# A second stage buffer, freer row buffers and a new static order in a graph-attention and slice-attention kernel

## The chip, the cores and the metric

The kernel runs on one core of a Trainium2 chip. The metric is the device time of one execution in microseconds (us). The core has five engines that matter here: TensorE (PE in the profile, with its weight loads as PEld), VectorE (DVE), ScalarE (ACT), GpSimd (POOL) and the queue of SyncE (SP), from which nearly all DMA transfers are issued.

## The reference, cut to what matters

x has 32 batches of 512 nodes with 256 features, all float32. Each batch is independent of the others; `adj` is shared. One layer is two residual blocks:

```python
def _gat(inp, adj_mask, W, a):
    h = inp @ W
    f1 = h @ a[:F_, 0];  f2 = h @ a[F_:, 0]
    e = leaky_relu(f1[:, :, None] + f2[:, None, :], 0.2)
    if adj_mask is not None:
        e = where(adj_mask > 0, e, NEG_INF)
    att = softmax(e, axis=2)
    return elu(einsum('bij,bjf->bif', att, h))

def gnn(x, ...):                                  # 256 -> 512 -> 256 features
    out = relu(x @ mlp1_w + mlp1_b);  residual = out
    out = elu(_gat(relu(out), None, W_fc, a_fc)) + residual
    out = relu(out @ mlp2_w + mlp2_b); residual = out
    return relu(elu(_gat(relu(out), adj, W_hand, a_hand)) + residual)

def ffn(x, ...):                                  # 8 heads, 64 slices of 64 features
    slice_weights = softmax((x_mid @ W_slice + b_slice) / temp)
    slice_token = einsum(fx_mid, slice_weights) / (sum(slice_weights) + 1e-5)
    # ... attention among the 64 slices of each head: q, k, v, softmax
    out_x = einsum(out_slice, slice_weights)
    return out_x @ W_out + b_out

x = x + gnn(layernorm(x), adj, ...)
x = x + ffn(layernorm(x), ...)
```

## The kernel before

The kernel does not run its instructions in the order in which they are written. `Recorder` first notes every operation of all 32 batches. It then gives each operation a key (the batch times a period, plus the turn of its step, plus corrections for the first three and the last three batches), and lays all operations out in one static order for each engine, with a list scheduler that starts, on each engine, the ready operation with the smallest key. Work of two to four batches is interleaved in this way. The chip then follows that fixed order, each engine by itself, and waits on semaphores where data or a buffer is not there yet.

A tile is given a buffer of its tag. The scheduler hands the buffers of a tag out in a fixed sequence of tiles: one sequence over all batches, or, for PSUM tiles and tags that begin with "stage", one sequence inside each batch, with the batches free against each other:

```python
class _Log:
    def __init__(self, ap, age):
        tensor = ap.tensor
        self.name, self.tag, self.bufs = tensor.name, tensor.tag, tensor.tag_meta.bufs
        self.psum = ap.space == bass.MemoryType.PSUM
        self.queue = self.tag, age if self.psum or self.tag.startswith("stage") else 0
```

`age` is the batch. The tiles `u` and `m` are rows of 512 elements with two buffers each; they serve in the first attention (pv) and in the second one (pv2). A tag carries the name of its pool after the tile's own, so the tags of these rows begin with "u_" and "m_".

A matrix is transposed either on TensorE, into PSUM, or in three parts: VectorE transposes 32x32 blocks into a stage tile (`flip`), four DMA transfers write the stage to DRAM, and one reads it back in the final order:

```python
EDGES = (0, B - 1)
Q = 32
def flip(src, dst):
    nc.vector.transpose(dst, src.rearrange("p (c i) -> p c i", i=Q))
def by_dma(what, b):
    return what in FLIPPED and b not in EDGES    # FLIPPED = xn, u, e, o2, w, xn2, s1
def gather(what, stage, dst):
    blocks, width = stage.shape[1:]
    scr = dram.tile([blocks, Q, P // Q, width], F32, name="scr", tag=f"scr_{what}", bufs=2)
    for a in range(P // Q):
        nc.sync.dma_start(scr[:, :, a, :].rearrange("c r j -> r c j"), stage[ts(a, Q), :, :])
    nc.sync.dma_start(dst, scr.rearrange("(k c) r a j -> (c r) k (a j)", c=P // Q))
```

The first and the last batch (`EDGES`) take TensorE's way instead, for all but o2. One batch goes through these steps (loops over tiles cut to one line, the TensorE branches for the edges cut):

```python
# load, norm1: xt from DRAM; layernorm on VectorE, with its power on GpSimd; xn flipped, gathered as xnT
# mlp1: 8 matmuls of 512 columns -> o0T (relu on ScalarE)
# h: 32 matmuls of 257 columns, weights wfc -> h (copies on ScalarE)
# factors, p: 5 transposes; two exponentials and four row products -> pT
nc.step = "pv"                               # first attention, 32 matmuls
o1T = new("o1T", [P, KH, N])
if by_dma("u", b):
    stage = new("u_stage", [P, HID // Q, P], tag="stage")
for i in range(NT):
    # ... pms: two PSUM tiles, pT x h
    u, m = row("u"), row("m")
    elu_elu([...], m, u)                     # VectorE and ScalarE in turn, 6 operations
    if by_dma("u", b):
        flip(u, stage[:, :, ts(i, Q)]); continue
nc.step = "o1"
gather("u", stage, o1T)
for m in range(KH):                          # + o0T, on VectorE
    nc.vector.tensor_tensor(o1, o1, swapped(o0T[:, m, :]), op=OP.add)

nc.step = "mlp2"                             # 8 matmuls of 512 columns
o2T = new("o2T", [P, KD, N])
# ... nc.scalar.activation(o2T[:, m, :], pm, AF.Relu, bias=...)
nc.step = "h2"                               # 8 matmuls of 258 columns, 4 transposes (f2b)
nc.step = "e"
if by_dma("e", b):
    stage = new("e_stage", [P, N // Q, P], tag="stage")
for i in range(NT):                          # 3 VectorE operations, exp on ScalarE, then:
    flip(e, stage[:, :, ts(i, Q)])
nc.step = "p2"
gather("e", stage, pT)                       # pT is p2T here
# ... o2T flipped and gathered as r2; x loaded again as x1
nc.step = "pv2"                              # second attention, 16 matmuls in two halves
u, m = row("u2", (P, 2, D), "u"), row("m2", (P, 2, D), "m")
# ... elu_elu, + r2, + x1

nc.step = "norm2"
layernorm(x1, xn, "ln2")                     # xn is xn2 here
raw = new("xn2_raw", [P, KD, N], tag="raw4")
transpose_features("xn2", b, xn, raw, True)  # 4 flips, gather; then ScalarE copies raw into xn2T
nc.step = "w"                                # 8 matmuls of 512 columns (weff, xn2T), softmax over 64
stage_w = new("w_stage", [P, INNER // Q, P], tag="stage")
# ... 4 flips; later gathered as w_raw and copied into wT
nc.step = "sums"                             # 16 matmuls of 257 columns (xn2, w) -> s1, flipped, gathered as s1T
nc.step = "tokens"                           # small matmuls: s1T x wfx, nrow x bfx, tok x wqk, scores (tok, qbd)
nc.step = "att"; "vo"; "gg"                  # softmax over 64 slices, transposes, attT x tokbd, 4 matmuls gg
attT = new("attT", [P, NP, G])
nc.step = "out"                              # 16 matmuls gg x wT, added to x1, written out
```

A DMA that is issued from the SP queue and has a wait stands in that queue until the wait is over; those behind it stand too.

Of the kernel before, what the change touches and what calls it, by code (L numbers as in the profile page):

```python
# [13 lines left out]
ENGINES = ("tensor", "vector", "scalar", "gpsimd", "sync")  # L14

TURNS = {
    "load": -145.1, "norm1": -102.2, "mlp1": 176.5, "h": 203.5, "factors": 206.6, "p": 209.3,
    "pv": 219.9, "o1": 240.0, "mlp2": 243.4, "h2": 273.9, "e": 274.6, "p2": 274.6,
    "pv2": 305.6, "norm2": 314.1, "w": 376.2, "sums": 378.3, "s1T": 396.3, "tokens": 446.2,
    "att": 472.7, "vo": 472.7, "gg": 472.7, "out": 483.8,  # L20
}
PERIOD, SPARE = 92.2, 0.00

HEAD = (
    (-8, -8, 49, -10, -8, 25, 0, -39, -4, 6, -2, -2, -40, -2, -2, -2, -2, -2, 3, -8, 1, -20),
    (8, 2, 25, 1, 1, 0, 8, 8, 1, 1, -7, 0, 2, 2, 2, 2, 2, 2, 2, -5, 9, 2),
    (0, -1, -1, 0, 0, -22, 0, 12, 0, 1, 0, 0, 0, 0, 0, 0, 11, 0, 0, 0, -3, 0),
)
TAIL = (
    (0, 0, 53, 0, 0, 0, 0, 4, 0, 0, -6, 2, 0, 0, 0, 0, 2, 0, 3, 3, -5, 4),  # L30
    (0, 0, 17, 1, -2, -27, 0, -2, -4, -38, 0, 23, 1, -6, -2, 9, 2, 6, -2, -2, -2, -2),
    (-85, 1, 1, 1, 1, 16, 20, 22, 19, 19, 19, 7, 14, -7, 9, 9, -7, 0, -7, 0, -16, -30),
)


# [2 lines left out]
FLIPPED = ("xn", "u", "e", "o2", "w", "xn2", "s1")  # L38

P = 128  # L40
# [235 lines left out]
# [5 lines that stand above are left out]
        self.name, self.tag, self.bufs = tensor.name, tensor.tag, tensor.tag_meta.bufs  # L281
        self.psum = ap.space == bass.MemoryType.PSUM

        self.queue = self.tag, age if self.psum or self.tag.startswith("stage") else 0
        self.entries = []


# [22 lines left out]
def adj_ffn_kernel(  # L310
# [26 lines left out]
    B, N, D = x.shape  # L337
    HID = mlp1_w.shape[1]
    HH = HID // 2
    NT = N // P  # L340
    KD = D // P
    KH = HID // P
    HEADS = temperature.shape[1]
    G = W_slice.shape[1]
    C = W_slice.shape[0]
    INNER = HEADS * C
    NP = INNER // P
# [11 lines left out]
    def new(name, shape, bufs=1, tag=None, dtype=F32):  # L359
        return sbuf.tile(list(shape), dtype, name=name, tag=tag or name, bufs=bufs)  # L360

    def mm_tile(shape):
        return psum.tile(shape, F32, tag="mm", name="mm", bufs=5)
# [4 lines left out]
    def sm_tile(shape):  # L368
        return tr_tile(shape)

    EDGES = (0, B - 1)
    Q = 32

    def flip(src, dst):
# [2 lines left out]

    def by_dma(what, b):

        return what in FLIPPED and b not in EDGES  # L380

    def gather(what, stage, dst):

# [32 lines left out]
    def load_x(b):  # L416
# [14 lines left out]
        out=ident, in_=ident, compare_op=OP.not_equal, fill=1.0, base=0,  # L431
# [160 lines left out]
    for p in range(NP):  # L592
        pv = mm_tile([P, D])
# [49 lines left out]
    def front(b):  # L643
# [5 lines left out]
        xn = new("xn", [P, NT, D])  # L649
# [15 lines left out]
        h = new("h", [P, NT, 2, HH + 1])  # L665
# [49 lines left out]
        nc.step = "pv"  # L715
        o1T = new("o1T", [P, KH, N])
        if by_dma("u", b):
            stage = new("u_stage", [P, HID // Q, P], tag="stage")
        for i in range(NT):
            pms = [mm_tile([P, HH + 1]), mm_tile([P, HH])]  # L720
            for s, pm in enumerate(pms):
# [7 lines left out]
            u, m = row("u"), row("m")  # L729
# [13 lines left out]
        if by_dma("u", b):  # L743
            gather("u", stage, o1T)
            for m in range(KH):
                o1 = o1T[:, m, :].rearrange("p (t a i) -> p t a i", t=NT, i=Q)
# [3 lines left out]
    def middle(b, o1T):  # L750

        nc.step = "mlp2"
        o2T = new("o2T", [P, KD, N])
        for m in range(KD):
            pm = mm_tile([P, N])
            for k in range(KH):
                nc.tensor.matmul(
                    pm.rearrange("p (a t i) -> p a t i", t=NT, i=Q), w2[:, k, ts(m)],
                    swapped(o1T[:, k, :]), start=(k == 0), stop=(k == KH - 1),
                )  # L760
            nc.scalar.activation(o2T[:, m, :], pm, AF.Relu, bias=b2[:, m : m + 1])
        nc.step = "h2"
        h = new("h2", [P, NT, D + 2])
        for t in range(NT):
            pm = mm_tile([P, D + 2])
            for k in range(KD):
                nc.tensor.matmul(
                    pm, o2T[:, k, ts(t)], wh[:, k, :], start=(k == 0), stop=(k == KD - 1)
                )
            nc.scalar.copy(h[:, t, :], pm)  # L770
        f2b = tr_tile([P, N])
        for j in range(NT):
            nc.tensor.transpose(f2b[:, ts(j)], h[:, j, D + 1 : D + 2].to_broadcast([P, P]), ident)
        if not by_dma("e", b):
            pt, f2b = f2b, new("f2b", [P, N], tag="acb")
            nc.scalar.copy(f2b, pt)
        nc.step = "e"
        pT = new("p2T", [P, NT, N])
        if by_dma("e", b):
            stage = new("e_stage", [P, N // Q, P], tag="stage")  # L780
        nmax = small("nmax", [P, NT])
        for i in range(NT):
            e = new("e", [P, N], bufs=2)
            nc.vector.scalar_tensor_tensor(
                e, f2b, h[:, i, D : D + 1], mbias[:, i, :], op0=OP.add, op1=OP.add
            )
            nc.vector.scalar_tensor_tensor(e, e, ALPHA, e, op0=OP.mult, op1=OP.max)
            nc.vector.tensor_reduce(
                nmax[:, i : i + 1], e, axis=AX.X, op=OP.max, negate=True
            )  # L790
            nc.scalar.activation(e, e, AF.Exp, bias=nmax[:, i : i + 1])
            if by_dma("e", b):
                flip(e, stage[:, :, ts(i, Q)])
                continue
            pt = tr_tile([P, NT, P])
            for j in range(NT):
                nc.tensor.transpose(pt[:, j, :], e[:, ts(j)], ident)
            nc.scalar.copy(
                pT.rearrange("p j (t a i) -> p j t a i", t=NT, i=Q)[:, :, :, i, :],
                pt.rearrange("p j (t i) -> p j t i", i=Q),  # L800
            )
        nc.step = "p2"
        if by_dma("e", b):
            gather("e", stage, pT)

        nc.vector.memset(h[:, :, D], 1.0)

        r2 = new("r2", [P, NT, D])
        stage = new("o2_stage", [P, N // Q, KD * Q], tag="stage4")
        for k in range(KD):  # L810
            nc.vector.transpose(
                stage[:, :, ts(k, Q)].rearrange("p (t a) i -> p t a i", t=NT),
                swapped(o2T[:, k, :]),
            )
        gather("o2", stage, r2)

        x1 = new("x1", [P, NT, D], bufs=2)
        nc.sync.dma_start(x1, x[b].rearrange("(p t) d -> p t d", p=P))
        nc.step = "pv2"
        for i2 in range(NT // 2):  # L820
            parts = []
            for s in range(2):
                i = 2 * i2 + s
                pm = mm_tile([P, D + 1])
                for j in range(NT):
                    nc.tensor.matmul(
                        pm, pT[:, j, ts(i)], h[:, j, : D + 1], start=(j == 0), stop=(j == NT - 1)
                    )
                rd = small("rd2", [P, 1])
                nc.vector.reciprocal(rd, pm[:, D : D + 1])  # L830
                parts.append((pm[:, :D], rd, s))
            u, m = row("u2", (P, 2, D), "u"), row("m2", (P, 2, D), "m")
            elu_elu(parts, m, u)
            for s in range(2):
                u3 = u[:, s, :].rearrange("p (k a i) -> p k a i", k=KD, i=Q)
                r3 = r2[:, 2 * i2 + s, :].rearrange("p (a k i) -> p k a i", k=KD, i=Q)
                nc.vector.tensor_tensor(u3, u3, r3, op=OP.add)
            nc.vector.scalar_tensor_tensor(
                x1[:, ts(i2, 2), :], u, 0.0, x1[:, ts(i2, 2), :], op0=OP.max, op1=OP.add
            )  # L840
        return x1

    def back(b, x1):

        nc.step = "norm2"
        xn = new("xn2", [P, NT, D + 1])
# [1 line left out]
        layernorm(x1, xn, "ln2")  # L848
        xnT = new("xn2T", [P, KD, N])
        if by_dma("xn2", b):  # L850
            raw = new("xn2_raw", [P, KD, N], tag="raw4")
            transpose_features("xn2", b, xn, raw, True)
            for k in range(KD):
                nc.scalar.copy(
                    xnT[:, k, :].rearrange("p (t a i) -> p t a i", t=NT, i=Q), swapped(raw[:, k, :])
                )
        else:
            transpose_features("xn2", b, xn, xnT, False)

        nc.step = "w"  # L860
        w = new("w", [P, NT, INNER])
        wT = new("wT", [P, NP, N])
        if by_dma("w", b):
            stage_w = new("w_stage", [P, INNER // Q, P], tag="stage")
        for t in range(NT):
            pm = mm_tile([P, INNER])
            for k in range(KD):
# [28 lines left out]
        s1 = new("s1", [P, NP, D + 1])  # L896
        if by_dma("s1", b):
            stage = new("s1_stage", [P, D // Q, P], tag="stage4")
# [20 lines left out]
        if by_dma("w", b):  # L919
            raw = new("w_raw", [P, NP, N], tag="w")  # L920
# [6 lines left out]
        s1T = med("s1T", (P, KD, INNER))  # L927
# [74 lines left out]
        pt = tr_tile([P, NP, G])  # L1002
        for q in range(NP // 2):
            nc.tensor.transpose(pt[:, ts(q, 2), :], sc[:, ts(q, 2), :], ident)
        attT = new("attT", [P, NP, G])
        nc.scalar.copy(attT, pt)
        pa = mm_tile([P, NP, G])
        halves(pa, tokbd, attT)
# [2 lines left out]
        gg = med("gg")  # L1011
        for p2 in range(NP // 2):
            pg = mm_tile([P, 2, D])
            for s in range(2):
                p = 2 * p2 + s
# [87 lines left out]
```

## Time and profile before

| | |
|---|---|
| time, median of 3 runs | 2681.41 us (2673.46 to 2681.55) |
| span of the profiled execution | 2673.3 us |
| DVE busy | 2081.2 us, 78% |
| ACT busy | 1093.4 us, 41% |
| DMA moved | 375.40 MB, mean 140 GB/s |
| TensorE busy in the first 84 us, in a middle stretch of 84 us, in the last 84 us | 68.8, 82.3 (918 to 1002 us), 68.6 us |

A line of the timeline has the start, the length, the engine, the source line (here always that of the recorder), the operation, the tile written and the tiles read, the shape, and how many such instructions follow each other. In square brackets stands the idle time of the engine just before, and what ended it. "SPq" is the queue of SyncE; its lines are issues of transfers, not the transfers. A float32 matmul as written in the kernel is two records in the trace, a transpose on TensorE is one. The profile leaves out some digits of tile names: `o_stage` is o2_stage, `xn_stage` stands for the stages of xn and of xn2, `xn_raw` is xn2_raw, `h` can be h or h2. `w_raw` is the gathered w before ScalarE copies it into wT; `mm` and `tr` are PSUM tiles. So `mm<-wfc,o0T` is the step h, `mm<-xnT,w` mlp1, `mm<-h,pT` pv, `mm<-o1T,w` mlp2, `mm<-wh,o2T` h2, `mm<-s1T,wfx` and `mm<-nrow,bfx` tokens, `mm<-tok,wqk` the step after them.

### The profile page before, as it was taken

To read this page: it belongs to the slowest core of one execution; us is meant where nothing else is said; L and a number is where in the kernel's file an instruction comes from. 1 tells how busy PE (TensorE), PEld (TensorE's weight loads), DVE (VectorE), ACT (ScalarE), POOL (GpSimd) and SP (SyncE) were. 2 spreads that over 40 slices of the span, in tenths; PEclk is the share of its full clock that TensorE was granted. 3 is DMA by queue.
4 is the path that set the end of the run, shared out by engine and by line. 5 is a ranking of instruction groups with operands and counts; after the bars stand their busy time and mean duration, and the time that the engine had idled before them with its cause. 6 is when DMAs were issued, how large, how long until landed. Compare 5 with 4: busy or idle time off the path is not lost.

```text
span 2673.3 us, 35248 instructions
## 1 busy us (share of the span) xinstructions
PE 2608.7 (98%) x12477; PEld 1929.1 (72%) x12477; DVE 2081.2 (78%) x5161; ACT 1093.4 (41%) x2009; POOL 111.8 (4%) x171
## 2 busy tenths in 40 slices
PE   7999999999999999999999999999999999999997
PEld 5776667777777777777777777776777767777775
DVE  6577778877778877779877788777788777888785
ACT  3443344433444433444434444334444334444341
POOL 1000000000000000000000000000000000000000
PEclk9999999999999999999999999999999999999998
DMA  5125455554455454556554555544564545554440
GB/s 162 52 67 148 122 156 166 152 156 132 137 166 166 137 161 116 147 168 165 148 141 128 157 166 148 154 127 139 168 172 134 154 122 150 166 158 142 127 119 23
DMA packets 465657, 375.40 MB, mean 140 GB/s; under 512 B 86597, under 2 KB 382665, under 8 KB 465481
## 3 DMA queue, kind: packets, MB, share of 16 engines
q1 hardware_dynamic: 463896, 372.10, 49.6%
q8 instruction: 99, 1.62, 0.2%
q10 hardware_dynamic: 1584, 1.05, 0.1%
q14 instruction: 78, 0.63, 0.1%
HBM read 197.96 MB, written 175.11 MB: 140 GB/s over the span
## 4 chain that ended last, share of the span: by engine, by line
PE 45%; DVE 29%; DMA 16%; issue 3%; SPq 3%; POOL 2%; ACT 1%; DVEq 0%; ACTq 0%
PE mm L273 43%; DMA xt<-in_x_dram 5%; DVE u L273 4%; DVE e L273 3%; DMA o1T<-scr 3%; DMA scr<-e_stage 3%; SPq L273 3%; PE tr L273 2%; DVE w L273 2%; POOL ln_rstd L273 2%; DVE e_stage L273 2%; DVE w_stage L273 2%; DMA scr<-u_stage 2%; DVE m L273 1%; DVE u_stage L273 1%
## 5 line engine op out<-in xcount | busy, mean ns | idle before, releaser
L273 PE MATMUL mm<-wfc,o0T 128*128 128x257 f32 x2048 | 479.3, 381 | 0.0
L273 PE MATMUL mm<-h,pT 128*128 128x257 f32 (+1 forms) x2048 | 468.1, 380 | 4.2 <-DVE pT L273 4.2
L273 PEld LDWEIGHTS mm<-wfc,o0T 128*128 128x128 f32 x2048 | 381.9, 189 | 82.2 <-issue 24.8
L273 PEld LDWEIGHTS mm<-h,pT 128*128 128x128 f32 x2048 | 385.2, 190 | 64.3 <-DVE pT L273 6.7
L273 ACT COPY h<-mm 128x257 f32<-128x257 f32 (+1 forms) x384 | 142.9, 372 | 302.2 <-PE mm L273 295.8
L273 PE MATMUL mm<-xn,w 128*128 128x257 f32 x1024 | 255.1, 383 | 4.0 <-ACT w L273 3.3
L273 PE MATMUL mm<-xnT,w 128*128 128x512 f32 x512 | 240.4, 600 | 10.8 <-DMA xnT<-scr 7.3
L273 PE MATMUL mm<-gg,wT 128*128 128x256 f32 x1024 | 245.3, 379 | 0.0
L273 PE MATMUL mm<-h,p2T 128*128 128x257 f32 x1024 | 244.9, 380 | 0.3 <-ACT o0T L273 0.3
L273 PE MATMUL mm<-o1T,w 128*128 128x512 f32 x512 | 227.4, 596 | 13.4 <-DVE o1T L273 10.8
L273 PE MATMUL mm<-weff,xn2T 128*128 128x512 f32 x512 | 231.7, 595 | 0.0
L273 PEld LDWEIGHTS mm<-h,p2T 128*128 128x128 f32 x1024 | 191.4, 190 | 31.3 <-ACT o0T L273 0.7
L273 PEld LDWEIGHTS mm<-xn,w 128*128 128x128 f32 x1024 | 187.8, 191 | 35.0 <-issue 8.9
L273 PEld LDWEIGHTS mm<-gg,wT 128*128 128x128 f32 x1024 | 191.7, 190 | 28.6 <-issue 1.0
L273 PEld LDWEIGHTS mm<-o1T,w 128*128 128x128 f32 x512 | 94.8, 190 | 131.0 <-issue 94.5
L273 DVE STREAM_TRANSPOSE o_stage<-o2T 128x512 f32<-128x512 f32 x64 | 45.5, 710 | 163.6 <-ACT o2T L273 163.6
L273 ACT ACTIVATE e<-e,nmax 128x512 f32<-128x512 f32 x128 | 92.4, 722 | 186.0 <-DVE nmax L273 184.5
L273 DVE SCALAR_TENSOR_TENSOR e<-tr,h,mbias 128x512 f32<-128x512 f32 x120 | 86.6, 742 | 99.3 <-PE tr L273 99.3
L273 ACT ACTIVATE m<-m 128x512 f32<-128x512 f32 x192 | 120.9, 630 | 102.4 <-DVE m L273 102.1
L273 PEld LDWEIGHTS mm<-weff,xn2T 128*128 128x128 f32 x512 | 93.0, 191 | 92.3 <-issue 90.5
L273 PEld LDWEIGHTS mm<-xnT,w 128*128 128x128 f32 x512 | 92.2, 191 | 93.1 <-issue 72.7
L273 ACT ACTIVATE w<-w 128x512 f32<-128x512 f32 x128 | 80.7, 631 | 177.2 <-DVE w L273 177.0
(151 smaller groups left out, 3798.9 us busy)
## 6 DMA issues: line engine op xcount, KB each, us to landing
scr<-xn_stage SPq DMA_DIRECT2D x240, 128.0 KB, 2.5
scr<-u_stage SPq DMA_DIRECT2D x120, 256.0 KB, 4.1
o1T<-scr SPq DMA_DIRECT2D x30, 1024.0 KB, 6.0
scr<-e_stage SPq DMA_DIRECT2D x120, 256.0 KB, 3.8
p2T<-scr SPq DMA_DIRECT2D x30, 1024.0 KB, 5.5
scr<-w_stage SPq DMA_DIRECT2D x120, 256.0 KB, 4.6
w_raw<-scr SPq DMA_DIRECT2D x30, 1024.0 KB, 7.3
x<-in_x_dram SPq DMA_DIRECT2D x32, 512.0 KB, 5.7
```

The costliest lines, as they stand in the source:

```text
L273: getattr(getattr(self.nc, op.engine), op.method)(*op.args, **op.kwargs)
```

## The change

It gives the three stage tiles of pv, e and w, which shared one buffer, two; lets the rows u and m of different batches be handed out independently of each other; and sends the first batch's w, xn2 and s1 through DRAM instead of through TensorE. To make room in SBUF, xn2_raw moves into the buffer of o2T, and attT into that of sc2. The turns of the steps and the corrections for the first and last three batches are set anew, so that the static order differs on each engine. The purpose is an order with fewer ties between batches.

```diff
 TURNS = {
-    "load": -145.1, "norm1": -102.2, "mlp1": 176.5, "h": 203.5, "factors": 206.6, "p": 209.3,
-    "pv": 219.9, "o1": 240.0, "mlp2": 243.4, "h2": 273.9, "e": 274.6, "p2": 274.6,
-    "pv2": 305.6, "norm2": 314.1, "w": 376.2, "sums": 378.3, "s1T": 396.3, "tokens": 446.2,
-    "att": 472.7, "vo": 472.7, "gg": 472.7, "out": 483.8,
+    "load": -122.2, "norm1": 78.3, "mlp1": 267.5, "h": 296.1, "factors": 313.0, "p": 323.7,
+    "pv": 324.8, "o1": 324.8, "mlp2": 340.5, "h2": 360.8, "e": 385.5, "p2": 385.7,
+    "pv2": 430.7, "norm2": 437.4, "w": 494.8, "sums": 496.8, "s1T": 507.4, "tokens": 549.1,
+    "att": 558.0, "vo": 558.2, "gg": 560.3, "out": 593.0,
 }
-PERIOD, SPARE = 92.2, 0.00
+PERIOD, SPARE = 91.1, 0.01
 # HEAD and TAIL: corrections of the keys of each step in the first and the last three batches,
 # 3 x 22 numbers each; before -85 to 53, after -478 to 149 (cut)
@@ class _Log
-        self.queue = self.tag, age if self.psum or self.tag.startswith("stage") else 0
+        self.queue = self.tag, age if self.psum or self.tag.startswith(("stage", "u_", "m_")) else 0
@@
-    EDGES = (0, B - 1)
+    EDGES = {0: ("xn", "u", "e"), B - 1: ("xn", "u", "e", "w", "xn2", "s1")}
@@ by_dma
-        return what in FLIPPED and b not in EDGES
+        return what in FLIPPED and what not in EDGES.get(b, ())
@@ pv
-            stage = new("u_stage", [P, HID // Q, P], tag="stage")
+            stage = new("u_stage", [P, HID // Q, P], bufs=2, tag="stage")
@@ e
-            stage = new("e_stage", [P, N // Q, P], tag="stage")
+            stage = new("e_stage", [P, N // Q, P], bufs=2, tag="stage")
@@ norm2
-            raw = new("xn2_raw", [P, KD, N], tag="raw4")
+            raw = new("xn2_raw", [P, KD, N], tag="o2T")
@@ w
-            stage_w = new("w_stage", [P, INNER // Q, P], tag="stage")
+            stage_w = new("w_stage", [P, INNER // Q, P], bufs=2, tag="stage")
@@ vo
-        attT = new("attT", [P, NP, G])
+        attT = new("attT", [P, NP, G], tag="sc2")
```

## The prediction

> **What bounds the kernel now.** I read the page's first two parts, then TensorE's timeline over one batch's period in the middle, then VectorE's and the DMA queue's timelines over the period before it, because an average over 32 batches does not tell which wait ends last.
>
> ```profile
> PE 2608.7 (98%) x12477; PEld 1929.1 (72%) x12477; DVE 2081.2 (78%) x5161; ACT 1093.4 (41%) x2009; POOL 111.8 (4%) x171
> ...
> PEclk9999999999999999999999999999999999999998
> DMA  5125455554455454556554555544564545554440
> ```
>
> TensorE looks full at full clock, but its busy time counts overlapping, modelled ends. The distance from one start to the next is the better ruler.
>
> ```profile
> 1108.82 1.90 PE L273 MATMUL mm<-wfc,o0T 128*128 128x257 f32 x8
> 1110.84 7.10 PE L273 MATMUL mm<-o1T,w 128*128 128x512 f32 x16
> ...
> 1159.61 12.71 PE L273 MATMUL mm<-h,pT 128*128 128x257 f32 x58
> 1172.25 1.15 PE L273 MATMUL mm<-s1T,wfx 128*64 128x64 f32 x32
> 1173.23 0.61 PE L273 MATMUL mm<-nrow,bfx 128*64 128x128 f32 x8
> 1174.07 1.10 PE L273 MATMUL mm<-xnT,w 128*128 128x512 f32 x2 [0.23 <-ACT m L273]
> 1175.33 0.70 PE L273 MATMUL mm<-tok,wqk 128*128 128x256 f32 x2 [0.16 <-DVE tok L273]
> ```
>
> Each matmul as written is two records, 0.215 us apart with 257 columns ((1172.25 - 1159.61)/58 = 0.218) and 0.43 with 512. Measured so, every period has three real gaps: nrow to xnT, xnT to tok, and h (wfc) to o1T. Over the 25 periods between 400 and 2400 us I take each start-to-start distance less the usual one of its shape: these three sum to 16.8, 5.3 and 14.7 us, or 0.67 + 0.21 + 0.59 = 1.47 us a period. A period is about 81.2 us (the x32 stretch of h in the chain that ended last begins at 460.94 and, 24 periods later, at 2411.01). So TensorE's own floor is about 79.8 us: 98% of the period. 81.2 x 32 is 2600; the other 73 us of the span are fill and drain.
>
> ```profile
> 1096.61 0.70 DVE L273 STREAM_TRANSPOSE u_stage<-u 128x512 f32<-128x512 f32 x1
> ...
> 1110.05 2.50 DVE L273 TENSOR_TENSOR o1T<-o1T,o0T 128x512 f32<-128x512 f32 x4 [0.34 <-DMA o1T<-scr]
> 1115.27 0.71 DVE L273 STREAM_TRANSPOSE o_stage<-o2T 128x512 f32<-128x512 f32 x1 [2.72 <-ACT o2T L273]
> 1118.70 0.71 DVE L273 STREAM_TRANSPOSE o_stage<-o2T 128x512 f32<-128x512 f32 x1 [2.72 <-ACT o2T L273]
> 1122.77 1.41 DVE L273 SCALAR_TENSOR_TENSOR e<-tr,h,mbias 128x512 f32<-128x512 f32 x2 [3.35 <-PE tr L273]
> ```
>
> ```profile
> 1097.34 3.10 SPq L273 DMA_DIRECT2D scr<-u_stage  x4
> 1100.48 3.49 SPq L273 DMA_DIRECT2D scr<-xn_stage  x4
> 1104.13 0.38 SPq L273 DMA_DIRECT2D o1T<-scr  x1
> 1106.22 0.38 SPq L273 DMA_DIRECT2D xn_raw<-scr  x1
> ```
>
> **The loop.** From the first e at 1122.77 VectorE runs with almost no idle until the last u flip, 55.3 us later (1178.06 in the next period). Its idle time, some 16 us a period, lies only between the attention and the next e. From the end of the last flip (1097.31) the o1T data need 12.7 us through DRAM (1110.05), then 0.8 us for the first addition, then 11.9 us of mlp2, h2 and transposes on TensorE (1110.84 to 1122.77). 55.3 + 12.7 + 0.8 + 11.9 = 80.7: this closed loop over VectorE, DMA and TensorE is as long as the period. It and TensorE's own work are both binding, and the o1T gap is where they meet.
>
> **The Trainium skill.** "Perfetto Trace Analysis", Identifying the Most-Contended Engine, says that matmul busy time is no measure of nearness to the limit; here 98% busy hides 1.47 us of gaps a period, so the trace agrees. Its Optimization Strategy says that a gap that repeats can mean too little SBUF for the next tile; the gaps do repeat, but here a lone stage buffer shows only indirectly, in the order it forces. "DMA: Bandwidth & Descriptors", Anatomy of one DMA, puts most of a fixed 2 us into completion and says that the waiting is done by the issuing sequencer; the trace has 2.5 us for a 128 KB store, and a queue that stands still until a store has landed. "VectorE: DVE Perf Modes", The three transpose paths, says that VectorE transposes 32x32 blocks only, which is why every flip (0.70 us for 128x512) is followed by a store and a gather.
>
> **The change, part by part.** The arithmetic is the same. Edge batch 0 loses 32 TensorE transposes (w 16, xn2 8, s1 8) at 0.109 us start to start, 3.5 us, and their copies out of PSUM; it gains flips and three DRAM trips, about 4 MB, when little else runs. I take 4 us gained, with a few us of new waits for DRAM possible in batch 0, which has no other batch's work to hide them.
>
> The order is what moves in the other batches. In the built program of the changed kernel the second half of pv2 (8 matmuls) stands behind pv, three mlp1 matmuls instead of one stand between nrow and wqk, and o1T is gathered before xn2 is stored. Let P be the end of pv.
> - TensorE from P to mlp2: pv2 3.45, tokens and nrow 1.43, mlp1 8 x 0.855 = 6.84, wqk 0.43, scores 0.62, transposes 0.27 + 0.22, att 0.62, gg 0.86, h 10 x 0.431 = 4.31: 19.05 us. Before, it was 17.75 us of work plus the 1.47 us of gaps.
> - VectorE's stretch from the first e to the last u flip loses the end of pv2 (u 0.6, two additions 0.75, x1 0.6, two statistics 0.7) and takes one gg in (0.6): 55.3 - 2.0 = 53.3 us. TensorE from the f2b transposes to P has 47.6 us by the same counting. The flip ends at P + 6.0, as before (1097.31 against 1091.38).
> - o1T: without the xn2 store's 3.5 us ahead of it in the queue the gather may go some 6.3 us after the flip and takes 5.9: P + 18.2, first addition P + 19.0. TensorE comes at 19.05. This gap closes, by a hair.
> - tok: ready at P + 6.5 behind the u flips; wqk comes at 3.45 + 1.43 + 2.57 = P + 7.45. Closed.
> - xnT: its flips end at about P - 3.5, and the trip took 7.5 us (1085.62 to about 1093.1): P + 4.0, against P + 4.9 wanted. But the w and s1 gathers (7.4 and 5.1 us) are closer now. I leave 0 to 0.8 us.
>
> The loop becomes 53.3 + 12.2 + 0.8 + 12.4 (one h inside) = 78.7, below TensorE's floor. If nothing new came, a period would win 1.4 us.
>
> **What may take it back.** xn2_raw moves into o2T's only buffer, so mlp2's first result can't be written before xn2_raw of the batch before has been copied out. x1's second half now follows pv2's end at P + 3.5; the normalisation waits for GpSimd's power (1.04 us) and stands among the attention's softmax steps; I count the last xn2 flip at P + 16.2 to 16.5. Store and gather took 7.5 us for xn and 11.4 us for xn2 (1099.91 to 1111.3, behind o1T's gather). With the cleaner queue I take 8 to 9: P + 25, copies 1.14, o2T 0.7 and signalling: P + 27. TensorE wants o2T for h2 at 19.05 + 6.84 + 0.43 = P + 26.3. So 0.5 to 1 us of wait at h2 is my middle, with 0 and 2 as the ends.
>
> Sum of a middle period: -1.47, +0.3 for xnT, +0.3 for the two ties, half of the h2 wait counted as +0.5 (a wait there also relaxes the ones upstream): -0.4 to -1.4, middle -1.0. The 29 full periods give -29 us, batch 0 -4 us, the end 0 (its TensorE gaps are 28 us in the last slice of 84 us; the changed order spreads the last out matmuls between the last batch's steps, but the final serial chain is unchanged). 2681.4 - 33 = 2648 us.
>
> **Rivals.** (1) A wait takes the gap's place: the o2T buffer holds up h2 by 2 us or more. For it: the 11.4 us trip above. Against: 16 us of idle VectorE time to absorb it. Then each period keeps its length or grows by up to 1 us: 2680 to 2710. (2) TensorE is the only bound and all three gaps close: 2681 - 29 x 1.47 - 4 = 2634, and 2615 if fill and drain gain too. For it: the loop sum. (3) The edges decide: the shifts of the first and last three batches are up to hundreds of us in the priority keys, so tail or head could lose 10 to 30 us, or win 10. Against: the printed order of the edges differs less than the numbers suggest. (4) Nothing is seen, since the gaps are 2% of the period: 2670 to 2680.
>
> **Range and chances.** All but rival 1's worst end and the edges' lie within 2% (2628 to 2735); only rival 2 with gains at the edges passes 2628. I take 2612 to 2695 as the range, faster by over 2%: 0.18, within: 0.76, slower: 0.06.
>
> **What would show it.** Right: a period of about 80.2 us; no idle before the mlp2 (o1T), xnT and wqk matmuls; a new idle of 0.5 us before h2, put down to ScalarE's o2T or the xn_raw transfer; 32 fewer transpose records; TensorE's busy time down by less than the span. Wrong: gaps at mlp2 as before (the loop isn't what I think), more than 1.5 us before h2 (rival 1), or a middle unchanged with the difference in the first 300 or last 120 us (rival 3).

## The result and the profile after

The changed kernel takes 2660.03 us (median of 4 runs, 2658.32 to 2661.68), the kernel before 2679.29 us (4 runs, 2673.46 to 2681.55). The ratio is 0.9931, with a 95% interval of 0.9912 to 0.9950: faster, by 19 us. The prediction was 2648 us, in a range of 2612 to 2695: the direction and the order of size were right, but the gain was put at 33 us.

The page of the changed kernel, first two parts:

```profile
PE 2603.5 (98%) x12445; PEld 1929.4 (73%) x12445; DVE 2098.5 (79%) x5173; ACT 1080.9 (41%) x2007; POOL 91.0 (3%) x171
...
PEclk9999999999999999999999999999999999999998
DMA  5245355554555454555544555545554545654440
```

TensorE has 32 records fewer, the transposes of the first batch, and shows 5.2 us less busy time while the span (2659.9 us against 2673.3) is 13.4 us shorter: the shares of busy time again hide where the time went. TensorE's timeline over one period in the middle shows it (start, length, operation, how many; idle before and its cause in brackets):

```profile
1107.81 7.13 PE L276 MATMUL mm<-o1T,w 128*128 128x512 f32 x16 [0.69 <-DVE o1T L276]
...
1115.22 3.65 PE L276 MATMUL mm<-wh,o2T 128*128 128x258 f32 x16
...
1155.50 1.13 PE L276 MATMUL mm<-h,pT 128*128 128x257 f32 x4 [0.18 <-DVE pT L276]
...
1156.58 11.85 PE L276 MATMUL mm<-h,pT 128*128 128x256 f32 x54
1168.26 3.64 PE L276 MATMUL mm<-h,p2T 128*128 128x257 f32 x16
1171.83 1.15 PE L276 MATMUL mm<-s1T,wfx 128*64 128x64 f32 x32
1172.81 0.61 PE L276 MATMUL mm<-nrow,bfx 128*64 128x128 f32 x8
1173.35 2.84 PE L276 MATMUL mm<-xnT,w 128*128 128x512 f32 x6
1176.03 0.59 PE L276 MATMUL mm<-tok,wqk 128*128 128x256 f32 x2
```

The second half of pv2 (`mm<-h,p2T` at 1168.26) now stands behind pv. The xnT records start 0.54 us after nrow instead of 0.84, and no wait is shown there, nor ahead of tok. The wait for o1T ahead of mlp2 is there in this period (0.69 us), but no longer in every one. h2 at 1115.22 waits for nothing. New is the wait for pT.

VectorE, and the DMA queue, over the same period:

```profile
1107.07 2.50 DVE L276 TENSOR_TENSOR o1T<-o1T,o0T 128x512 f32<-128x512 f32 x4 [1.97 <-DMA o1T<-scr]
1120.21 1.41 DVE L276 SCALAR_TENSOR_TENSOR e<-tr,h,mbias 128x512 f32<-128x512 f32 x2 [3.79 <-PE tr L276]
...
1154.72 0.73 DVE L276 SCALAR_TENSOR_TENSOR pT<-acb,ex,pT 128x512 f32<-128x512 f32 x1
...
1173.77 0.70 DVE L276 STREAM_TRANSPOSE u_stage<-u 128x512 f32<-128x512 f32 x1
```

```profile
1108.59 0.38 SPq L276 DMA_DIRECT2D xn_raw<-scr  x1
...
1174.50 3.09 SPq L276 DMA_DIRECT2D scr<-u_stage  x4
1181.69 0.38 SPq L276 DMA_DIRECT2D o1T<-scr  x1
1184.72 1.29 SPq L276 DMA_DIRECT2D scr<-xn_stage  x3
```

The last pT product ends at 1155.45 and pv goes on at 1155.50: TensorE waited for it. The gather of o1T is issued 7.2 us after the last u flip ends (1174.47), ahead of the stores of xn2.

One period can be cut into legs, which are read from such timelines in each of 22 periods and averaged (us): from the start of mlp2 to the first e, on to the end of the last pT product, on to the end of pv, on to the end of the last u flip, on to the issue of o1T's gather, on to the first o1T addition, on to the next mlp2.

| leg | before | changed |
|---|---|---|
| mlp2 to first e (TensorE) | 11.92 | 12.35 |
| first e to last pT (VectorE) | 36.69 | 35.24 |
| last pT to end of pv (TensorE) | 12.76 | 12.82 |
| end of pv to last u flip (VectorE, ScalarE) | 5.98 | 6.65 |
| last u flip to issue of the gather (store) | 6.97 | 6.72 |
| issue to first o1T addition (gather) | 6.16 | 5.53 |
| first addition to mlp2 | 0.80 | 1.22 |
| period | 81.28 | 80.53 |

The last leg tells most. Before, it is 0.79 to 0.80 us in 21 of the 22 periods: mlp2 starts as soon as the addition allows, so the trip of u through DRAM set every period, and each delay of a transfer went into the time. After, it is 0.75 us in about half of the periods and up to 1.93 us in the others, where TensorE came later than the data. The chain of work that ended last, followed back over the whole span, says the same. Before, then after:

```profile
PE 45%; DVE 29%; DMA 16%; issue 3%; SPq 3%; POOL 2%; ACT 1%; DVEq 0%; ACTq 0%
```

```profile
PE 72%; DVE 14%; DMA 7%; ACT 3%; issue 2%; SPq 1%; POOL 0%; DVEq 0%; ACTq 0%
```

TensorE's gaps, taken as the prediction took them (25 periods between 400 and 2400 us, us a period):

| gap ahead of | before | changed |
|---|---|---|
| xnT (mlp1), behind nrow | 0.67 | 0.20 |
| tok (wqk) | 0.21 | 0.01 |
| o1T (mlp2) | 0.59 | 0.24 |
| pv, for pT | 0.03 | 0.32 |
| h2, for o2T | 0.00 | 0.01 |
| all, with the small ones between 64-column matmuls | 4.38 | 3.72 |

The 0.20 us left ahead of xnT is not a wait: in the changed kernel the distance from the last nrow record to xnT is 0.202 or 0.203 us in all 25 periods, while before it was 0.36 to 1.29 us. This distance of the two shapes stands in both columns, so the real gap was 0.47 us before and is closed now.

Over the profile: the 23 periods from batch 5 to batch 28 got 0.757 us shorter each, 17.4 us together; the time up to mlp2 of batch 5 grew from 460.9 to 462.1 us, and that from batch 28 to the end from 343.2 to 346.1 us. -17.4 + 1.2 + 2.9 = -13.3 us. The profiled execution of the kernel before was among its quickest, and that of the changed kernel was the slowest of its four, so the medians show more.

### The profile page after: what moved, and what is told of

It is laid out like the page before. It is cut to its first block, busy times and chain, and to the rows that moved or that the text cites. A ratio compares the mean times of both kernels' runs of the same rounds, so it can differ in the third digit from the quotient of the medians.

```text
span 2659.9 us, 35389 instructions
## 1 busy us (share of the span) xinstructions
PE 2603.5 (98%) x12445; PEld 1929.4 (73%) x12445; DVE 2098.5 (79%) x5173; ACT 1080.9 (41%) x2007; POOL 91.0 (3%) x171
## 4 chain that ended last, share of the span: by engine, by line
PE 72%; DVE 14%; DMA 7%; ACT 3%; issue 2%; SPq 1%; POOL 0%; DVEq 0%; ACTq 0%
PE mm L276 70%; PE tr L276 3%; DVE pT L276 3%; DMA w_raw<-scr 2%; DMA o1T<-scr 2%; DMA scr<-u_stage 1%; DVE s L276 1%; DVE s_stage L276 1%; ACT m L276 1%; DVE w L276 1%; DVE u L276 1%; DVE w_stage L276 1%; SPq L276 1%; ACT acb L276 1%; DVE acb L276 1%
## 5 line engine op out<-in xcount | busy, mean ns | idle before, releaser
L276 PE MATMUL mm<-wfc,o0T 128*128 128x257 f32 x2048 | 493.1, 381 | 0.0
L276 ACT ACTIVATE u<-mm,rd 128x256 f32<-128x256 f32 x192 | 89.4, 467 | 279.3 <-PE mm L276 160.2
L276 DVE SCALAR_TENSOR_TENSOR u<-m,u 128x512 f32<-128x512 f32 x192 | 129.6, 686 | 34.8 <-ACT m L276 33.2
```

Source lines behind the costliest of these rows:

```text
L276: getattr(getattr(self.nc, op.engine), op.method)(*op.args, **op.kwargs)
```

## Experiments

All edits that move or add single instructions are made behind the scheduler, in the loop that emits its list, so that every other instruction keeps its place. Ratios are to the kernel before, measured beside it.

**1. One swap in the DMA queue of the kernel before**

```diff
+# in each middle batch: o1T's gather ahead of the four xn2 stores on SyncE
+while seq[j - 1].step == "norm2": j -= 1
+seq.insert(j, seq.pop(g))
```

> The kernel before, with one thing of the change's order and nothing else: in each middle batch the gather of o1T stands ahead of the four stores of xn2 in the DMA queue. Loop theory (the middle period is a closed loop of VectorE's stretch from the first e to the last u flip, the DRAM trip of u, the first o1T addition and mlp2 to the next e, on average 55.43 + 13.13 + 0.80 + 11.92 = 81.28 us): the trip falls from 13.1 to about 12.3 us, as in the changed kernel, and the time with it, by 0.6 to 0.9 us in each of some 29 periods: 15 to 25 us less, most of the change's gain. Rival (the gain comes from VectorE's shorter stretch and from TensorE's matmuls being placed elsewhere; the queue order is a detail): within 5 us of before. Second rival (xn2, now later in the queue, holds up ScalarE and with it o2T and h2): slower by 10 us or more.

Measured: 2671.28 us, ratio 0.9969 (0.9958 to 0.9981), 8 us faster. That is less than either number of the loop theory and more than its rival's. The queue of this kernel:

```profile
1094.80 3.09 SPq L284 DMA_DIRECT2D scr<-u_stage  x4
1101.16 0.38 SPq L284 DMA_DIRECT2D o1T<-scr  x1
1101.58 2.48 SPq L284 DMA_DIRECT2D scr<-xn_stage  x4
```

The gather goes out 6.4 us after the first store of u, against 6.8 before (1097.34 to 1104.13): it was hardly waiting for the xn2 stores, but for u's own stores to land. In the profile that is worth 0.1 us a period; the runs say 0.29 (8.3 us over 29 periods). So it is part of the gain, but not the main part.

**2 and 3. The same load on and off the way**

```diff
+# before the last u flip of a batch (2), or before the copy into meanbd (3)
+nc.vector.tensor_reduce(dum, mbias[:, 0, :], axis=AX.X, op=OP.max)
```

> The kernel before, with one more VectorE instruction in each of 30 batches, a maximum over 512 elements of a constant tile (about 0.6 us), right ahead of the last u flip; nothing waits for its result. Loop theory: the load lies on the loop, so the time grows by 30 x 0.6 = 18 us (12 to 20). Rival (TensorE's work sets the period, and VectorE, at 78 percent, has room): within 3 us of before.

> The kernel before, with the same additional VectorE instruction of about 0.6 us in each of 30 batches, but right ahead of the copy into meanbd, where VectorE sat idle for 2.35 us. Loop theory: within 3 us of before. Rival (every microsecond of VectorE's work counts, wherever it stands): as much slower as with the load ahead of the u flip, some 18 us.

Measured: 2709.55 us, ratio 1.0109 (1.0093 to 1.0125), and 2689.59 us, ratio 1.0032 (1.0020 to 1.0044). The added instruction takes 0.679 us. The two kernels differ only in its place, by 20.0 us (15 to 26 by the two intervals), and 30 x 0.679 is 20.4: ahead of the u flip nearly all of it reaches the end. But the load in the idle place cost 10 us as well, which neither theory says. Both kernels show the same excess elsewhere: the leg from the first e to pT grew by 0.31 us, and the four stores of u took 3.38 us to issue instead of 3.10. In that leg VectorE's wait for the load of the next x (`xt`) grew from 0.28 to 0.6 us a period, so both excesses come by way of the transfers. Why these are slower is open: both kernels hold one more small tile than the kernel before, so other tiles may lie elsewhere in SBUF, but that was not tried apart.

**4. Less VectorE work, behind pT**

```diff
+if op.step == "pv2" and op.method == "tensor_tensor" and 0 < op.age < 31:
+    continue                      # the residual is left out of the output
```

> The kernel before, with the four residual additions of the second attention left out in 30 batches (about 4 x 0.37 = 1.5 us of VectorE's stretch from the first e to the last u flip in each batch; the output lacks the residual). Everything else stays in its order. Loop theory: the loop gets 1.5 us shorter, and TensorE's work becomes the bound once its gaps are closed, so the gain stops between the gap ahead of mlp2 alone (0.59 us a period, 17 us) and all three gaps (1.47 us a period, 43 us). Rival (the loop isn't what binds): within 5 us of before.

Measured: 2673.24 us (22 runs), ratio 0.9974 (0.9965 to 0.9984), 7 us faster. The 1.5 us that left VectorE shortened its stretch from the first e to the last u flip by 0.33 us only (55.43 to 55.10): these additions stand behind pT, where the next thing to end is pv on TensorE, and the leg from the first e to the end of pv stayed at 49.46 us. The profiled run shows no gain at all: its period is 81.28 us as before, and TensorE waits 0.86 us a period ahead of mlp2 instead of 0.59. Where the 7 us come from is open. The prediction's loop was wrong in one point: VectorE's dense look in that stretch does not make it the bound of all of it.

**5. One stage buffer again**

```diff
-            stage = new("u_stage", [P, HID // Q, P], bufs=2, tag="stage")
+            stage = new("u_stage", [P, HID // Q, P], tag="stage")        # e and w too
```

> The changed kernel with the stage tiles of pv, e and w in one buffer again; all else of the change stays, and the scheduler again puts the second half of pv2 behind pv. Window theory (what matters is how much of TensorE's work stands between the end of pv and mlp2, where the trip of u through VectorE and DRAM takes about 20 us; before it was 17.8 us, now 19.1): the order keeps that, so nearly all of the gain stays, 2655 to 2668 us. Rival (the second stage buffer takes away a tie between u, e and w): the gain is lost, 2672 to 2685 us.

Measured: 2793.71 us, ratio 1.0442 (1.0427 to 1.0456). Both guesses were far off, and two things are in it. The first batches fall apart: the second batch's mlp2 starts at 250.7 us instead of 142.7, because the scheduler, with keys meant for two buffers, lays whole steps of the first batch bare one behind the other:

```profile
169.87 2.01 PE L276 MATMUL mm<-xn,w 128*128 128x257 f32 x8 [0.97 <-DVE s L276]
...
182.89 1.98 PE L276 MATMUL mm<-s1T,wfx 128*64 128x64 f32 x32 [9.77 <-DMA s1T<-scr]
```

And the middle period is 81.47 us, 1 us longer than the changed kernel's 80.51, although pv2's second half still stands behind pv. So that placement alone isn't the gain, as the window theory had it. The leg from the first e to pT is even 1.0 us shorter than in the changed kernel. What got longer is the way from there to the last u flip (19.5 to 21.1 us), where VectorE waits 1.4 us a period instead of 0.4 for ScalarE's exponentials of u, and the leg from mlp2 to the first e (by 0.6 us). Which of these the second buffer does by itself was not separated.

**6. The first batch through TensorE again**

```diff
-    EDGES = {0: ("xn", "u", "e"), B - 1: ("xn", "u", "e", "w", "xn2", "s1")}
+    EDGES = {0: ("xn", "u", "e", "w", "xn2", "s1"), B - 1: ("xn", "u", "e", "w", "xn2", "s1")}
```

> The changed kernel with the first batch's w, xn2 and s1 through TensorE again; the order of the middle is the same but for the first few batches. Theory of the prediction (32 transposes of 0.109 us and their copies saved): 4 us slower than the changed kernel. Rival (the first batch now waits for DRAM, and the time up to batch 5 grew by 1.2 us in the profile): 0 to 5 us faster than the changed kernel.

Measured: 2663.57 us, ratio 0.9949 (0.9936 to 0.9963), against 0.9931 (0.9912 to 0.9950) for the whole change. 3.5 us by the medians, close to the predicted 4, but the intervals overlap: likely, not shown. The profiles agree: mlp2 of batch 5 starts at 465.1 us instead of 462.1.

**7. Rows in one sequence again**

```diff
-self.tag.startswith(("stage", "u_", "m_"))
+self.tag.startswith("stage")
```

> The changed kernel with the rows u and m handed out in one sequence over all batches again. The scheduler then cannot put pv of a batch between the halves of pv2 of the batch before; with the new turns its order falls back to whole steps one behind the other (nrow, wqk, scores, transposes, att, gg with no other matmul between). Window theory and its reading that the free rows make the new order possible: the waits of that bare chain, about 8 us in the last batch of the kernel before, come back in every batch: 2850 us or more. Rival (the free rows are a detail beside the second stage buffer): within 15 us of the changed kernel.

Measured: 4147.38 us, ratio 1.5506 (1.5485 to 1.5527). The new turns without the free rows give an order in which the batches hardly overlap; the middle period is 127 us, and in the middle of the run TensorE is busy for three quarters of the time, at a mean granted clock of 0.84 instead of 1.00. The line gives the stretch and its length, the busy time and number of instructions of TensorE, its weight loads, VectorE, ScalarE and GpSimd, then the clock, the DMA share and GB/s:

```profile
1000.00:2000.00 1000.00, 744.95 (x3039) 515.35 (x3040) 522.67 (x1256) 261.25 (x489) 21.88 (x40) 0.84 0.35 96
```

**8. The old turns on the new buffers**

```diff
-TURNS, PERIOD, SPARE, HEAD, TAIL   # of the changed kernel
+TURNS, PERIOD, SPARE, HEAD, TAIL   # of the kernel before
```

> The changed kernel's buffers and first batch, with the turns and corrections of the kernel before. The scheduler puts all of pv2 ahead of pv's main part, as before, and 8 h matmuls more or fewer around mlp2. Window theory: the gap ahead of mlp2 comes back, 2672 to 2695 us. Rival (buffers alone bring the gain, the turns only follow): 2655 to 2668 us.

Measured: 2779.60 us, ratio 1.0389 (1.0375 to 1.0403), period 85.1 us. Both guesses missed: it is not the gap ahead of mlp2 that came back (0.26 us a period, as in the changed kernel), but new ones came around tokens, which the scheduler now splits with pv. Experiments 5, 7 and 8 say the same: buffers and turns are one piece. Each half with the other's partner is worse than either kernel, so they can't be credited apart.

**9 to 11. Two single edits on the kernel before, and both**

```diff
+# 9: three h matmuls from behind f2b to ahead of mlp2, TensorE alone, 23 batches
+moved = [op for op in pe[m:] if op.age == age + 1 and op.step == "h"][:3]
+# 10: the two additions of out on VectorE left out, 30 batches (the second block's result is missing)
+if op.step == "out" and op.engine == "vector" and 0 < op.age < 31: continue
+# 11: both
```

> The kernel before, with one move on TensorE in 23 middle batches: three h matmuls (1.29 us) that stood behind f2b stand ahead of mlp2, where TensorE waits for o1T. Nothing else moves. Between the end of pv and mlp2 TensorE then has as much work as in the changed kernel. Two ties (from the first e to the last pT VectorE needs 36.7 us in every period, and TensorE's own work up to that place takes just as long; both have to become shorter): the gap of 0.59 us ahead of mlp2 closes, but pv now waits 1.3 us for pT instead, so the time stays within 4 us of before. Rival (the filled window alone is the gain): 12 to 17 us faster.

> The kernel before, with the two additions of the step out on VectorE left out in 30 batches (2 x 0.6 = 1.2 us between the first e and the last pT; the output lacks the second block's result). Two ties: pT is ready 1.2 us earlier, but TensorE's own work up to pv is as long as before, so the time stays within 5 us of before. Rival (the prediction's closed loop, with VectorE's stretch as the bound): 17 to 35 us faster.

> Both edits together in the kernel before: three h matmuls ahead of mlp2 in 23 batches, and the two additions of out left out in 30. Two ties: only now both legs up to pv are shorter, by 1.2 to 1.3 us, and the 20 us from the end of pv to mlp2 stay: 0.6 to 1.3 us less in each of 23 periods, 14 to 29 us faster, more than the two alone add up to. Rival (the effects are separate): the sum of the two alone.

Measured: 2694.09 us, ratio 1.0035 (1.0025 to 1.0045); 2675.08 us, ratio 0.9960 (0.9946 to 0.9974); 2680.28 us, ratio 0.9990 (0.9978 to 1.0002). None of the three is what the two ties say: 9 was to stay within 4 us and is some 10 us slower, 10 was to stay within 5 us and is 7 us faster by the medians (its profiled period, 81.24 us, is that of before), and 11 is refuted: both together brought nothing. The waits of TensorE tell why for 9 and 11. Of 9 (in total, times, longest):

```profile
PE mm L281 <- ACT w L281: 18.4, 25, 2.4
```

In 11 the same wait has the same three numbers; before, it was 3.3 us in 2 places. In TensorE's timeline of 9 it stands in the middle of out and sums:

```profile
1113.30 3.20 PE L281 MATMUL mm<-wfc,o0T 128*128 128x257 f32 x14
1116.34 7.03 PE L281 MATMUL mm<-o1T,w 128*128 128x512 f32 x16
...
1143.05 1.10 PE L281 MATMUL mm<-xn,w 128*128 128x257 f32 x4 [0.66 <-ACT w L281]
```

The gap ahead of mlp2 is closed (mlp2 begins 3.04 us after h's 14 records began, which is their own cadence), as the window theory wanted. But the sums now come before w's softmax is through VectorE and ScalarE: 1.06 us a period, taken back and more. Of this, 0.79 us stand ahead of the first sum and stay in 11. The other 0.27 us, ahead of the sums of w's last quarter, are gone in 11: of the two additions of out that it leaves out, one stands on VectorE ahead of that quarter's last product, the other behind it. So the tie that I had put at pT stands at w already, between the first e and pT. VectorE's stretch and TensorE's work run side by side with several ties between them, all with nearly no slack.

**12. One more step on the changed kernel**

```diff
+# VectorE, batches 3 to 30: the s1 flip and the statistics between the third and the
+# fourth pT product go behind the fourth
+moved = dve[ps[2] + 1 : ps[3]]
```

> The changed kernel, with the last of the four pT products moved ahead of one s1 flip and one statistics on VectorE (0.66 us) in batches 3 to 30; nothing else moves. The changed kernel waits 0.32 us a period for this product. Theory that this wait is part of the period: 5 to 9 us faster than the changed kernel, 2651 to 2655 us. Rival (the u trip behind pv sets the period anyway, or the later s1 flip holds something up): within 3 us of the changed kernel, or slower.

Measured: 2653.20 us, ratio 0.9879 (0.9864 to 0.9895); the changed kernel has 0.9931 (0.9912 to 0.9950), so this is faster than both. In its timeline the two products follow each other, and pv no longer waits for them:

```profile
1147.11 1.40 DVE L284 SCALAR_TENSOR_TENSOR pT<-acb,ex,pT 128x512 f32<-128x512 f32 x2
```

```profile
1148.44 0.60 PE L284 MATMUL mm<-h,p2T 128*128 128x257 f32 x2
1148.88 1.03 PE L284 MATMUL mm<-h,pT 128*128 128x257 f32 x4
1149.94 0.27 PE L284 MATMUL tr<-ident,s 128*4 128x128 f32 x1
```

The wait for pT is gone (0.00 us a period after 0.32), the leg to pT is 34.60 us, the period 80.27 us. A part comes back, 0.19 us a period ahead of the transpose of s (1149.94), because VectorE ends its write of s at 1149.89 only. Here a single move paid. My reading is that behind this tie there was room: the changed order has slack at mlp2 (1.22 us in the last leg, where 0.75 is the least) and no wait at w, so the next tie did not take the gain back.

Not tried: pv2's second half ahead of pv in the changed kernel, with all else kept. The PSUM tiles are handed out in the other order, so that such an order would stand still. What that placement is worth by itself stays open.

## Why the prediction held, step by step

- **Which gaps close.** Predicted: tok closed, o1T "closes, by a hair", xnT 0 to 0.8 us. Measured: tok 0.01, o1T 0.24 and xnT 0.00 us, with the fixed distance taken off. Right, and the hair was real: o1T still makes TensorE wait in some periods. But the three gaps before were 1.27 us a period, not 1.47, because the working took the 0.20 us of fixed distance for a gap, and TensorE's floor was about 80.0 us.
- **The wait that comes in return.** Predicted: 0.5 to 1 us ahead of h2, from the buffer that xn2_raw and o2T now share, with the last xn2 flip at P + 16.2 to 16.5. The flip ends at P + 16.4 (1184.69 against 1168.26), and ScalarE is indeed late with o2T, as its timeline shows:

```profile
1112.32 1.14 ACT L276 COPY xn2T<-xn_raw 128x512 f32<-128x512 f32 x2 [6.42 <-DMA xn_raw<-scr]
1113.49 0.69 ACT L276 ACTIVATE o2T<-mm,b 128x512 f32<-128x512 f32 x1
1114.99 0.69 ACT L276 ACTIVATE o2T<-mm,b 128x512 f32<-128x512 f32 x1 [0.81 <-PE mm L276]
```

  The first o2T starts the moment the copies are over. But it ends at 1114.18, a microsecond before h2 wants it at 1115.22, since mlp2 itself begins later than counted: at P + 20.1 by the last four legs of the table, not P + 19.05. This term was 0.5 in the sum and is 0.01. What took its place I had not named: the wait for pT, 0.32 us, and 0.1 us within pv. The step that failed is the place of the returning wait; that its size was near is luck.
- **The loop.** Predicted: 55.3 + 12.7 + 0.8 + 11.9 before, with VectorE's stretch shrinking by 2.0 us and the trip by 0.5. Measured: the stretch 55.43 to 54.71 us, 0.72 shorter; the trip (store and gather) 13.13 to 12.25 us, 0.88 shorter. The additional h in the way to the next e cost 0.43 us, as counted. The stretch is where the working failed. VectorE's work in it did shrink, by 2.4 us, but I summed its instructions as if it were never idle, and its idle time there rose from 0.9 to 2.5 us a period. In the new order it waits for ScalarE's exponentials (0.79 us ahead of the first e flip, 0.31 us ahead of a u row in the period shown), and experiment 4 shows that work taken out of this stretch need not shorten it. On the other hand, experiments 2 and 3 show that the part from pv to mlp2 is on the way nearly in full, 20.0 us for 20.4 us of load.
- **The sum of a period.** Predicted -1.0 us in each of 29 periods, measured -0.76 in the 23 between batch 5 and batch 28: 23 x 0.24, or 5.6 us short.
- **The edges.** Predicted -4 us for the first batch and 0 for the end. Experiment 6 puts the first batch's part at 3.5 us (not clear of its uncertainty), but the new order loses elsewhere: in the profiles the time up to batch 5 is 1.2 us longer, not shorter, and the end is 2.9 us longer. With the six full periods that lie there the prediction had -10 us for the two, measured are +4.1: 14 us short, the larger part of the 20 us by which the gain in the profiles, 13.3 us, misses 33. So the edges were mis-sized most, and rival 3 was partly right. The saved transposes were lost to waits: TensorE's idle time grew from 23.0 to 26.6 us up to mlp2 of batch 5, and from 18.8 to 20.6 us behind that of batch 28. Which step of the order brings them was not tried apart.

So the mechanism was right in its core for the middle periods: TensorE's own work was nearly the bound, the remaining gaps were ties to u's trip, to xnT and to tok, and the new order loosened them while making one new, smaller one. What stays open is how much each of the four ingredients (second buffer, free rows, turns, queue order) would be worth with turns set for it alone; the runs show only that the queue order alone is worth 8 us, and that these turns and these buffers don't work without each other. The change also lays tiles out otherwise in SBUF. The four stores of u took 3.10 us to issue before and after, so the slowing of experiments 2 and 3 is not seen, but what the layout is worth was not tried.

## What to carry to other kernels

When a tuned kernel's engine is 98% busy, cut a middle period into legs and look for the leg with no spread: here first addition to mlp2, 0.80 us in nearly every period, said that the transfer ahead of it set the pace. Where two engines run side by side with several exact ties, moving one instruction only moves the wait to the next tie (experiments 9 and 11), so order has to change on both sides; once there is slack, a single move can pay again (experiment 12). A static order and the buffers that it was made for are one design: half of it may be far worse than none.

## What was not expected of the hardware

A VectorE instruction in a place where the engine sat idle for 2.35 us made the kernel 10 us slower, together with one more small tile in SBUF: the four 256 KB stores of u took 3.38 instead of 3.10 us to issue, and VectorE's leg to pT 0.31 us more. The kernel before spread over 13.5 us in 28 runs (2672.94 to 2686.47), and its median moved from 2675.5 to 2682.4 us between sets of runs, which were on different chips. Whether the transfers that it waited for in each period make this spread was not shown. So ratios to runs made beside it were needed for effects under half a per cent.
